# Filling one edge tile's source columns on a second engine (ScalarE, one group in 24) in place of its gather

## The chip, the cores and the metric

The kernel runs on one core of one Trainium2 chip. The metric is device time in microseconds (us). The core's engines appear in the profile as PE (TensorE matmul), PEld (its weight load), DVE (VectorE), ACT (ScalarE), POOL (GpSimd) and SP (SyncE, which issues DMAs). Each works off its own queue of instructions in order, and they wait for one another on semaphores.

## The reference

One layer of a message-passing graph network over N = 12500 nodes with 64 features and E = 212500 edges, which come sorted by destination. Everything is fp32.

```
msg_in   = concat(x[src], x[dst], edge_attr)            # 64 + 64 + 32
messages = relu(msg_in @ mW1 + mb1) @ mW2 + mb2
agg      = segment_sum(messages, dst, N)
u        = relu(concat(x, agg) @ uW1 + ub1) @ uW2 + ub2
out      = layernorm(x + u)
```

## The kernel before

**Tiles and groups.** The edges are cut into tiles of 128 and groups of three tiles (384 edges), which makes G = 554 groups. As the edges are sorted, the destinations of a group lie in a window of 32 nodes. A second path for inputs that break this is in the program behind a branch and isn't taken here.

**A group's path.** `gather(g)` (L143, POOL) issues one indirect DMA for each tile: it brings the 64 features of the 128 sources into a slot of the ring `own.s` (20 slots, one edge per partition). `onehot(g)` (L322, DVE) writes beside them, for each edge, which of the 32 window nodes it goes to. Then three PE parts follow. `turn(g)` (L352) transposes the three tiles into PSUM, and ScalarE copies the result to `own.st` (L364), where the 32 edge features of the group have been loaded below it (L282, SP). `hidden(g)` (L384) multiplies this with the weights `own.wm`, whose middle 32 rows hold the window's share (`windows`, L308 and L313), and ScalarE's relu writes `own.h` (L393). `sums(g)` (L411, L414) sums the messages of the window with the one-hot columns, and VectorE adds the sums to `agg` (L423) and the counts to a row of `xc` (L424), the table of all nodes with features on partitions.

**The order of work.** It is written out by hand. Iteration k of the main loop issues, in this order: on SP some loads; every fourth time the next four windows (`places`, L294 and L301 on DVE); `onehot(k + 1)`; one PE step that holds `turn(k)`, `hidden(k - 2)` and `sums(k - 4)`, and every fourth time the windows' matmul, followed by ScalarE's copy of k and relu of k - 2, and VectorE's sums of k - 4; `gather(k + 16)`; and `copies_of(k)`. The last instruction of a PE step alone raises the semaphore that the copy, the relu and the sums wait for. PSUM holds two steps, so that step k + 2 starts when VectorE has read step k. The first gather of a group waits until ScalarE's copy of the group 20 before it has freed the ring's slot. Every 512 finished nodes an update round (L441 to L475) is put between the steps, 25 in all.

**The copied tile.** In every 16th group from 44 on (`COPIED`, 31 groups), the last tile isn't gathered. VectorE copies its sources' columns out of `xc`, one node at a time, into `own.f` (L341: 64 partitions by 1 element), over the 16 iterations that end four before the group's own (`SPREAD`, `LEAD`): eight columns in an iteration, after eight indices have been loaded into registers (L336, one TENSOR_LOAD for eight). This tile needs no transposing of features: `hidden` multiplies `own.f` and the 32 lower rows separately (two matmuls in place of one), and the copy to `own.st` is made in two pieces, 64 rows by 256 and 32 rows by 384:

```
parts = [(slice(0, D + W), n)]
if g in COPIED:
    parts = [(slice(0, D), n - P), (slice(D, D + W), n)]
```

Of the kernel before, what the change touches and what calls it, by code (L numbers as in the profile page):

```python
# [13 lines left out]
AF = mybir.ActivationFunctionType  # L14
ALU = mybir.AluOpType
ET = mybir.EngineType
# [3 lines left out]
P = 128  # L20
N = 12500
E = 212500
D = 64
# [8 lines left out]
G = (E + GE - 1) // GE  # L32
# [10 lines left out]
BITS = 16  # L43
NEAR_GROUPS = 24
SHORT = 10
EVERY = 16
COPIED = range(44, G - 16, EVERY)
ONE = TG - 1
SPREAD = 16
LEAD = 19  # L50
REGS = 8
TIMES = 4

# [1 line left out]
def tiles_of(g):  # L55

    n = min(GE, E - g * GE)
    return [min(P, n - j * P) for j in range((n + P - 1) // P)]
# [23 lines left out]
class Own:  # L82
# [4 lines left out]
    def __init__(self, nc, ctx):  # L87
        def on(name, *shape, of=nc.sbuf_tensor):
            return ctx.enter_context(of(name, list(shape), F32)).ap()

        self.s = [on(f"own_s{i}", P, TG, D + W) for i in range(RING)]
        self.st = [on(f"own_st{i}", P, SB * GE) for i in range(BLOCKS)]
        self.wm = [on(f"own_wm{i}", P, H) for i in range(NW)]
        self.h = [on(f"own_h{i}", P, TG, H) for i in range(NH)]

        self.f = [on(f"own_f{i}", P, P) for i in range(2)]
        self.ident = on("own_ident", P, P)
        self.counts = on("own_counts", D + W, G)

        self.ps = [on(f"own_ps{i}", P, 3, 512, of=nc.psum_tensor) for i in range(2)]  # L100
# [3 lines left out]
def ordered(ctx: ExitStack, tc: tile.TileContext, a, own, ok):  # L104
# [3 lines left out]
    nc = tc.nc  # L108
# [9 lines left out]
    def copied(g, j):  # L118
        return g in COPIED and j == ONE

# [3 lines left out]
    nc.sync.dma_start(src_sb[:, :first], a["src"][:, :first])  # L124

    loads, places_by, copy_by, relu_by, sums_by, wm_by, turn_by = ({} for _ in range(7))
    efs_by, hidden_by, columns_by, ahead = {}, {}, {}, []

    def after(first, *others):

        tc.declare_no_dep(first.ins, group="quiet", reason="waits for the last of a step")
        for i in others:
            tc.add_manual_dep(
                first.ins, i.ins.name,
                mybir.DependencyInfo(mybir.DependencyClass.Sync, mybir.DependencyReason.DATA),
                reason="the kernel's own rings",
            )
        return first
# [27 lines left out]
    zero = const.tile([P, NP // P], F32, name="zero")  # L166
    nc.vector.memset(zero, 0.0)
    nc.vector.tensor_copy(ident, ident_t)
    for t in own.f:
        nc.vector.memset(t[D:, :], 0.0)  # L170
    iota = iop.tile([P, W], F32, name="iota")
    nc.vector.tensor_copy(iota, iota_i)
# [2 lines left out]
    xc = const.tile([D + 2, NP], F32, name="xc")  # L175
# [24 lines left out]

    cols_sb = const.tile([len(COPIED), P], I32, name="cols_sb")
    nc.sync.dma_start(cols_sb, a["src_rows"])
# [82 lines left out]
    def columns(g):  # L285
        t, c = own.st[g // SB % BLOCKS], (g % SB) * GE
        return t, c, sum(tiles_of(g))
# [31 lines left out]
    def onehot(g):  # L319
# [5 lines left out]
        )  # L325
        after(places_by[g], *([sums_by[g - RING]] if g >= RING else []))

    def copies_of(k):

        for i, g in enumerate(COPIED):  # L330
            at = k - (g - LEAD)
            if not 0 <= at < SPREAD:
                continue
            for r in range(at * P // SPREAD, (at + 1) * P // SPREAD):
                if r % REGS == 0:
                    _, ahead[:] = nc.values_load_multi_w_load_instructions(  # L336
                        cols_sb[i : i + 1, r : r + REGS], engines=[ET.DVE], min_val=0,
                        max_val=N - 1,
                        skip_runtime_bounds_check_because="a source is one of the nodes",
                    )  # L340
                c = nc.vector.tensor_copy(own.f[i % 2][:D, r : r + 1],  # L341
                                          xc[:D, bass.ds(ahead[r % REGS], 1)])
                after(c, *([hidden_by[COPIED[i - 2]]] if i > 1 else []))
                columns_by[g] = [c]

    def turn(g, ps):
# [9 lines left out]
        def copy(step):  # L356
            t, c, n = columns(g)
            turn_by[g] = step
# [3 lines that stand above are left out]
# [11 lines left out]
    def hidden(g, ps):  # L373
        t, c, n = columns(g)
        sizes = tiles_of(g)
        pre = ps[:, 1, : TG * H].rearrange("p (j h) -> p j h", h=H)
        did, w = [], wm[g % NW]
        for j, p in enumerate(sizes):
            cols = t[:, c + j * P : c + j * P + p]
            parts = [(cols, w)]  # L380
            if copied(g, j):
                parts = [(own.f[COPIED.index(g) % 2], w), (cols[D:, :], w[D:, :])]
            for i, (edges, weights) in enumerate(parts):
                did.append(nc.tensor.matmul(pre[:p, j, :], edges, weights, start=i == 0,  # L384
                                            stop=i == len(parts) - 1))
        needs = [copy_by[g], wm_by[g], efs_by[g // SB], *(wm_loads[g] if g < NW else ()),
                 *columns_by.pop(g, [])]

        def relu(step):
            hidden_by[g] = step  # L390
            h = own.h[g % NH]
            if len(set(sizes)) == 1:
                relu_by[g] = [nc.scalar.activation(h, pre, AF.Relu)]  # L393
            else:
                relu_by[g] = [nc.scalar.activation(h[:p, j, :], pre[:p, j, :], AF.Relu)
                              for j, p in enumerate(sizes)]
            for i in relu_by[g]:
                after(i, step, *([sums_by[g - NH]] if g >= NH else []))
            return relu_by[g]

        return did, needs, relu
# [80 lines left out]
    def step_update(g):  # L482
# [5 lines left out]
        elif now:  # L488
            got = now[1](now[0])
            now = [got, *now[2:]] if len(now) > 2 else []  # L490

    users = {part: [[], []] for part in (turn, hidden, sums)}

    def step(*work):
# [33 lines left out]
    for k in range(G):  # L528
        if k < BITS:
            bit(k)  # L530
        if k % SB == 2:
            inputs(k // SB + 2)
        if k % SB == 1:
            places(k // SB + 1)
        onehot(k + 1)
        if k < G - SHORT:
            step((turn, k), *([(hidden, k - 2)] if k > 1 else []),
                 *([(sums, k - 4)] if k > 3 else []))
            made, summed = max(0, k - 1), max(0, k - 3)
        else:  # L540

            step((turn, k))
            for _ in range(2):
                if summed < made:
                    step((sums, summed))
                    summed += 1
            for _ in range(2):
                if made <= k:
                    step((hidden, made))
                    made += 1  # L550
        if k + AHEAD < G:
            gather(k + AHEAD)
        copies_of(k)
# [285 lines left out]
@with_exitstack  # L839
def gnn_layer(ctx: ExitStack, nc, a):  # L840
    own = Own(nc, ctx)
    tc = ctx.enter_context(tile.TileContext(nc))
    flag = ctx.enter_context(tc.tile_pool(name="flag", bufs=1))
    ok = flag.tile([1, 1], I32, name="ok")
    with tc.manual_schedule():
        ordered(tc, a, own, ok)
    good = nc.values_load(ok[0:1, 0:1], min_val=0, max_val=1,
                          skip_runtime_bounds_check_because="a comparison's result")
    with tc.If(good == 0):
        with tc.manual_schedule():  # L850
            unordered(tc, a)
# [36 lines left out]
```

## Time and profile before

| | |
|---|---|
| three runs | 2655.7, 2661.27, 2664.23 us; median 2661.27 |
| the profiled execution | 2655.7 us; its span, first to last instruction, 2654.0 us |
| mean granted TensorE clock | 0.786 of full speed |
| busy share of the span | PE 64%, POOL 58%, PEld 55%, DVE 40%, ACT 21% |
| gathers (L143) | 1630, 944 ns each |
| columns copied (L341) | 3968, 144 ns each |

In the profile's rows, "idle before" is the time for which the engine did nothing just ahead of the instruction, with the event that ended it behind an arrow; "issue" there means that the profile shows no event for it. A matmul in fp32 counts as two instructions. The timeline's rows give the start, the duration, the engine, the line, the operation, the tiles, and how many instructions were merged into one row; a merged row's duration is that of all of them.

### The profile page before, as it was taken

How to read it: one execution, taken by the hardware profiler on the slowest of the kernel's cores; microseconds unless marked ns; L12 is line 12 of the kernel's file. 1: busy time of each engine (PE TensorE's matmuls, PEld its weight loads, DVE VectorE, ACT ScalarE, POOL GpSimd, SP SyncE). 2: the span in 40 equal slices, each digit the busy share in tenths (PEclk: the TensorE clock that was granted, in tenths of full speed). 3: DMA queues.
4: the chain of work that ended last, by engine and by line, in shares of the span. 5: the costliest groups of instructions: out<-in, count | busy, mean ns of one | idle time of the engine just before them, and what ended most of it. 6: DMA issues, size and time to landing. Idle time of an engine off the chain costs nothing. (4 is left out here: it accounts for less than half of the span.)

```text
span 2654.0 us, 39223 instructions
## 1 busy us (share of the span) xinstructions
PE 1694.0 (64%) x9503; PEld 1466.6 (55%) x9503; DVE 1061.8 (40%) x7161; ACT 563.0 (21%) x1746; POOL 1539.8 (58%) x1637
## 2 busy tenths in 40 slices
PE   0366666666666766666666766657666666666677
PEld 0355555555555655555565655556555555555565
DVE  4124344343443443434434434444344343443423
ACT  0112222221222221222212222222222222222222
POOL 7565555565555655565556555655555555565550
PEclk9677788777777877787877778887777878887779
DMA  3221111111111111111111111111111111111110
GB/s 75 59 46 37 35 33 38 30 37 32 36 34 35 33 37 31 37 33 35 37 33 36 34 34 34 35 35 34 36 32 38 31 37 32 36 35 35 35 33 15
DMA packets 72472, 95.61 MB, mean 36 GB/s; under 512 B 32956, under 2 KB 40378, under 8 KB 72234
## 3 DMA queue, kind: packets, MB, share of 16 engines
q0 software_dynamic: 52160, 53.49, 10.7%
q1 hardware_dynamic: 19160, 39.05, 5.3%
q8 instruction: 81, 1.33, 0.2%
q14 instruction: 157, 1.29, 0.2%
q10 hardware_dynamic: 914, 0.46, 0.1%
HBM read 89.58 MB, written 3.20 MB: 35 GB/s over the span
## 5 line engine op out<-in xcount | busy, mean ns | idle before, releaser
L143 POOL DMA_INDIRECT own_s<-in_x,src_sb x1630 | 1539.0, 944 | 1039.1 <-ACT own_st L364 584.1
L352 PE MATMUL own_ps<-own_ident,own_s 128*96 128x128 f32 x1661 | 373.0, 348 | 864.1 <-issue 737.4
L352 PEld LDWEIGHTS own_ps<-own_ident,own_s 128*96 128x96 f32 x1661 | 227.5, 161 | 943.6 <-issue 802.5
L364 ACT ACTIVATE own_st<-own_ps 96x384 f32<-96x384 f32 (+2 forms) x585 | 280.3, 479 | 1935.5 <-PE own_ps L414 1062.0
L414 PE MATMUL own_ps<-own_s,own_h 128*128 128x128 f32 x3322 | 654.3, 346 | 0.9 <-issue 0.9
L384 PE MATMUL own_ps<-own_wm,own_st 128*128 128x128 f32 (+1 forms) x3322 | 633.5, 341 | 1.4 <-DVE own_wm L313 1.4
L384 PEld LDWEIGHTS own_ps<-own_wm,own_st 128*128 128x128 f32 (+1 forms) x3322 | 582.3, 256 | 11.7 <-issue 6.3
L423 DVE TENSOR_TENSOR agg<-own_ps,agg 128x32 f32 x554 | 105.8, 191 | 1187.9 <-ACT own_h L393 1025.8
L414 PEld LDWEIGHTS own_ps<-own_s,own_h 128*128 128x128 f32 x3322 | 531.5, 238 | 27.9 <-issue 0.6
L341 DVE COPY own_f<-xc 64x1 f32 x3968 | 430.1, 144 | 216.6 <-issue 212.2
L393 ACT ACTIVATE own_h<-own_ps 128x384 f32<-128x384 f32 x553 | 264.3, 478 | 17.8 <-PE own_ps L384 13.0
L313 DVE COPY own_wm<-own_ps 32x128 f32<-32x128 f32 x550 | 157.0, 285 | 5.7 <-issue 0.2
L322 DVE TENSOR_TENSOR own_s<-iota,dlc 128x96 f32<-128x96 f32 x554 | 135.8, 246 | 13.7 <-issue 8.2
L424 DVE TENSOR_TENSOR xc<-own_ps,xc 1x32 f32 x554 | 101.1, 183 | 26.7 <-PE u_ps L442 5.1
L411 PE MATMUL own_ps<-own_ident,own_counts 32*1 32x32 f32 x554 | 107.2, 193 | 3.8 <-ACT own_st L364 1.9
L364 ACT ACTIVATION_READ_ACCUMULATOR own_st<-own_ps 96x1 f32 (+1 forms) x554 | 107.2, 194 | 0.7
L301 DVE COPY xw<-xc 66x32 f32 x554 | 76.3, 202 | 48.9 <-issue 45.5
L411 PEld LDWEIGHTS own_ps<-own_ident,own_counts 32*1 32x1 f32 x554 | 41.1, 74 | 95.1 <-issue 50.6
L454 PE MATMUL u_ps<-u,u 128*128 128x64 f32 (+1 forms) x196 | 49.1, 401 | 18.0 <-ACT u L444 15.6
L454 PEld LDWEIGHTS u_ps<-u,u 128*128 128x128 f32 (+1 forms) x196 | 47.2, 324 | 20.0 <-ACT u L444 17.2
L308 PE MATMUL own_ps<-w1b,xw 66*128 66x128 f32 (+1 forms) x276 | 57.2, 291 | 0.0
L308 PEld LDWEIGHTS own_ps<-w1b,xw 66*128 66x128 f32 (+1 forms) x276 | 45.7, 207 | 0.1
(62 smaller groups left out, 261.0 us busy)
## 6 DMA issues: line engine op xcount, KB each, us to landing
own_st<-in_efT SPq DMA_DIRECT2D x138, 192.0 KB
own_s<-in_x,src_sb POOLq DMA_INDIRECT x1630
xin<-in_x SPq DMA_DIRECT2D x24, 128.0 KB
out<-o SPq DMA_DIRECT2D x24, 128.0 KB
xc<-in_xT SPq DMA_DIRECT2D x12, 179.2 KB
dlc_i<-in_dst_cols SPq DMA_DIRECT2D x1, 831.0 KB
xc<-in_xT SPq DMA_DIRECT2D x4, 179.5 KB
src_sb<-in_src SPq DMA_DIRECT2D x13, 50.5 KB
```

Source lines behind the costliest of these rows:

```text
L143: nc.gpsimd.indirect_dma_start(out=s[:p, j, :D], out_offset=None, in_=x[:, :], in_offset=bass.IndirectOffsetOnAxis(ap=src_sb[:p, g * TG + ...
L308: did = nc.tensor.matmul(wp[: n * W, :], xw[:, :n, :], w1b, start=True, stop=True)
L313: c = nc.vector.tensor_copy(wm[g % NW][D : D + W, :], wp[i * W : (i + 1) * W, :])
L322: places_by[g] = nc.vector.tensor_tensor(own.s[g % RING][:, :, D:], iota.unsqueeze(1).to_broadcast([P, TG, W]), dlc[:, g * TG : (g + 1) * ...
L341: c = nc.vector.tensor_copy(own.f[i % 2][:D, r : r + 1], xc[:D, bass.ds(ahead[r % REGS], 1)])
L352: nc.tensor.transpose(xt[:, j * P : j * P + p], s[:p, j, :], ident[:p, :p])
L364: nc.scalar.activation(t[to, c : c + m], xt[to, :m], AF.Copy, **({"accum_out": counts[to, g : g + 1]} if to.stop > D else {})), step)
L384: did.append(nc.tensor.matmul(pre[:p, j, :], edges, weights, start=i == 0, stop=i == len(parts) - 1))
L393: relu_by[g] = [nc.scalar.activation(h, pre, AF.Relu)]
L411: did = [nc.tensor.transpose(line, counts[lo:, g : g + 1], ident[lo : D + W, lo : D + W])]
L414: did.append(nc.tensor.matmul(sg, h[:p, j, :], s[:p, j, D:].unsqueeze(1).to_broadcast([p, TIMES, W]), start=j == 0, stop=j == len(sizes) - 1))
L423: after(nc.vector.tensor_tensor(agg[:, at], sg[:, 0, :], agg[:, at], ALU.add), step),
```

## The change

A second set of groups is copied in place of gathered: every 24th from 48 on, 21 groups, none of which is in the first set. Their columns are copied by ScalarE, with an activation of the kind Copy, over the 24 iterations that end four before the group's own: 128 / 24, so five or six columns in an iteration, behind that iteration's relu in ScalarE's queue. ScalarE loads the indices into its own registers, eight at a time. Each engine has its own pair of tiles in `own.f`. VectorE's groups, and where its copies stand, stay as they were. The changed kernel has 1609 gathers, 3968 column copies on VectorE and 2688 on ScalarE, and 336 register loads on ScalarE.

```
-EVERY = 16
-COPIED = range(44, G - 16, EVERY)
 ONE = TG - 1
-SPREAD = 16
-LEAD = 19
+BY_DVE = range(44, G - 16, 16)
+BY_ACT = range(48, G - 16, 24)
+COPIED = {**dict.fromkeys(BY_DVE, (ET.DVE, BY_DVE)), **dict.fromkeys(BY_ACT, (ET.Activation, BY_ACT))}
+SLACK = 3
...
-        self.f = [on(f"own_f{i}", P, P) for i in range(2)]
+        self.f = {way: [on(f"own_f{len(way)}_{i}", P, P) for i in range(2)]
+                  for way in (BY_DVE, BY_ACT)}
...
+    def source_columns(g):
+        _, way = COPIED[g]
+        return own.f[way][way.index(g) % 2]
+
     def copies_of(k):
 
-        for i, g in enumerate(COPIED):
-            at = k - (g - LEAD)
-            if not 0 <= at < SPREAD:
+        for n, (g, (engine, way)) in enumerate(COPIED.items()):
+            at = k - (g - SLACK - way.step)
+            if not 0 <= at < way.step:
                 continue
-            for r in range(at * P // SPREAD, (at + 1) * P // SPREAD):
+            f, used, ahead = source_columns(g), g - 2 * way.step, held[engine]
+            for r in range(at * P // way.step, (at + 1) * P // way.step):
                 if r % REGS == 0:
                     _, ahead[:] = nc.values_load_multi_w_load_instructions(
-                        cols_sb[i : i + 1, r : r + REGS], engines=[ET.DVE], min_val=0,
+                        cols_sb[n : n + 1, r : r + REGS], engines=[engine], min_val=0,
                         max_val=N - 1,
                         skip_runtime_bounds_check_because="a source is one of the nodes",
                     )
-                c = nc.vector.tensor_copy(own.f[i % 2][:D, r : r + 1],
-                                          xc[:D, bass.ds(ahead[r % REGS], 1)])
-                after(c, *([hidden_by[COPIED[i - 2]]] if i > 1 else []))
+                column = f[:D, r : r + 1], xc[:D, bass.ds(ahead[r % REGS], 1)]
+                c = (nc.vector.tensor_copy(*column) if engine == ET.DVE
+                     else nc.scalar.activation(*column, AF.Copy))
+                after(c, *([hidden_by[used]] if used in way else []))
                 columns_by[g] = [c]
...
-                parts = [(own.f[COPIED.index(g) % 2], w), (cols[D:, :], w[D:, :])]
+                parts = [(source_columns(g), w), (cols[D:, :], w[D:, :])]
```

More of the change, by code (lines that the diff above doesn't have):

```diff
@@ L126, in ordered @@
     loads, places_by, copy_by, relu_by, sums_by, wm_by, turn_by = ({} for _ in range(7))
-    efs_by, hidden_by, columns_by, ahead = {}, {}, {}, []
+    efs_by, hidden_by, columns_by = {}, {}, {}
+    held = {ET.DVE: [], ET.Activation: []}
     def after(first, *others):
@@ L168, in ordered @@
     nc.vector.tensor_copy(ident, ident_t)
-    for t in own.f:
+    for t in [t for pair in own.f.values() for t in pair]:
         nc.vector.memset(t[D:, :], 0.0)
```

## The prediction

> **What bounds the kernel now.** I read the page's busy times and costliest groups first, then the waits, then the timeline of two stretches. The chain of waits covers only the last 100 us, so it says nothing about the loop.
>
> ```profile
> span 2654.0 us, 39223 instructions
> PE 1694.0 (64%) x9503; PEld 1466.6 (55%) x9503; DVE 1061.8 (40%) x7161; ACT 563.0 (21%) x1746; POOL 1539.8 (58%) x1637
> ...
> L143 POOL DMA_INDIRECT own_s<-in_x,src_sb x1630 | 1539.0, 944 | 1039.1 <-ACT own_st L364 584.1
> L352 PE MATMUL own_ps<-own_ident,own_s 128*96 128x128 f32 x1661 | 373.0, 348 | 864.1 <-issue 737.4
> ```
>
> No engine is full. PE idles 864 us ahead of its turns, and POOL idles 584 us for ScalarE's copy, so the gathers don't starve PE: counted over the trace's rows, PE's turn of a group starts about 84 us after the group's last gather was issued. Yet POOL matters, as the timeline shows:
>
> ```profile
> 1314.70 0.94 POOL L143 DMA_INDIRECT own_s<-in_x,src_sb  x1 [2.34 <-ACT own_st L364]
> ...
> 1319.68 0.94 POOL L143 DMA_INDIRECT own_s<-in_x,src_sb  x1 [0.30 <-issue]
> ...
> 1320.92 0.94 POOL L143 DMA_INDIRECT own_s<-in_x,src_sb  x1 [0.30 <-issue]
> 1320.98 0.94 PE L414 MATMUL own_ps<-own_s,own_h 128*128 128x128 f32 x6
> 1323.33 0.49 ACT L364 ACTIVATE own_st<-own_ps 96x384 f32<-96x384 f32 x1 [6.14 <-PE own_ps L414]
> ...
> 1324.17 0.94 POOL L143 DMA_INDIRECT own_s<-in_x,src_sb  x1 [2.31 <-ACT own_st L364]
> 1324.18 0.48 ACT L364 ACTIVATE own_st<-own_ps 96x384 f32<-96x384 f32 x1
> ...
> 1327.31 0.26 DVE L322 TENSOR_TENSOR own_s<-iota,dlc 128x96 f32<-128x96 f32 x1
> ...
> 1327.64 0.45 PEld L352 LDWEIGHTS own_ps<-own_ident,own_s 128*96 128x96 f32 x3 [5.92 <-issue]
> ```
>
> POOL issues six gathers, 1.25 us apart, and stops for the ring. Meanwhile PE has finished two steps, the first (with L308) at 1319.42 and the second at 1321.92, but ScalarE gets the first's signal only at 1323.33, some 1.4 us after POOL's last gather ended (1320.92 + 0.94). Counted over the trace's semaphore records: of the 244 steps whose matmuls ended 4 to 8 us into a streak of six gathers, 2 signalled at once; the others' signals came together about 8.6 us after the streak's start. Of 52 that ended in a streak's first 1.5 us, 50 signalled at once. Once the gathers are over, nothing is held:
>
> ```profile
> 2578.77 0.90 POOL L143 DMA_INDIRECT own_s<-in_x,src_sb  x1 [0.30 <-issue]
> ...
> 2581.84 0.94 PE L414 MATMUL own_ps<-own_s,own_h 128*128 128x128 f32 x6
> ...
> 2582.81 0.49 ACT L364 ACTIVATE own_st<-own_ps 96x384 f32<-96x384 f32 x1 [1.56 <-PE own_ps L414]
> ```
>
> So the loop is a lockstep. Two steps are released, POOL gathers two groups (7.2 us), the next signals come 1.4 us later, and copy and wake-up take 0.85. There are 276 such stalls for 554 groups, and between groups 60 and 520 a group takes 4.68 us. Inside this, a second loop runs nearly as long: release, copy, relu (1.0 us), VectorE's sums, its column copies, the one-hot (to 1327.57), PE's next turn (1327.64), whose step may end only at the streak's end.
>
> **Term 1, the gathers left out.** 21 gathers at 1.25 us are 26.2 us of POOL's time, if nothing else becomes late. The 31 tiles copied already show what is kept. I cut the trace at the turns of k divisible by 4; all copied groups, old and new, are divisible by 4. By how far ahead the copied group lies, four steps take 17.77 us (20 groups ahead: the streak with five gathers), 18.87 (24), 18.58 (28) and 19.56 (16, where another copied group is itself turned). Against 18.72, the mean of the two neutral cycles, a missing gather saves 0.95 us: 21 x 0.95 = -20 us.
>
> **Term 2, the copied group's own step.** The cycle of 19.56 loses 0.84. The rows explain it: ScalarE's copy comes in two pieces (376 and 482 ns for one of 485) on the path to the release, and PE makes four instructions in place of two for that tile (2 x 394 + 2 x 465 for 2 x 339 ns, 1.04 us more). 21 x 0.84 = +18 us. Terms 1 and 2 thus nearly cancel. With 27 cycles of each kind and a spread of 1.4 us, each mean is good to 0.27, so their sum is -2 +- 8 us.
>
> **Term 3, the columns on ScalarE.** 2688 copies and 336 register loads are spread over 504 iterations: 5.33 copies each, and a load in two of three. No such copy is in the trace on ScalarE. From below, VectorE's spacing holds, eight in 0.95 us, so 0.12 each; from above, ScalarE's smallest ACTIVATE (L463, 297 ns), nothing overlapped. I take about 0.15, nearer to the lower row, since ScalarE's read of the accumulator already starts 0.1 us before its copy's recorded end. A register load costs VectorE 0.9 us between its neighbours (L424's end to the next L341) and here about 0.75, as part of it runs under the relu. An iteration's block is thus 0.9 us (six, no load) to 1.5 us (five with a load); at the upper row 1.8 to 2.2.
>
> What is queued behind the block is the next step's copy and relu, and behind these POOL's ring and VectorE's sums. Where two signals come together, the second copy moves from 0.85 us after the release to between 1.7 and 2.4. POOL asks for it after three more gathers, 0.85 + 3.75 = 4.6 us (3.35 if the streak has lost one): covered. VectorE asks for the second relu once it is through with sums (0.4), columns (1.85) and one-hot (0.25) of the first, from 1.0 on: 3.5 us after the release. The relu is done at 0.85 + 0.9 to 1.5 + 0.97 = 2.7 to 3.3. So the cover is VectorE's own column block, and 0.2 to 0.8 us of it are left. In windowed steps 1.2 us more of L313 cover it; in a stretch without VectorE's columns the block would show whole. The stalls scatter by about 0.6 us (1.5 to 2.8 between their tenth and ninetieth percentile), so I let one in four of the 168 second steps that have a load be late by 0.3 us: +13 us. With the upper row 168 steps would be late by about 0.45 us: +76. From below it is 0: I see no gain in it, as nothing is taken off an engine that others wait for.
>
> [...]
>
> **Edits at nothing.** ScalarE's first column waits for the DMAs of `xc`; the last of these was issued at 148 us, and iteration 21 starts near 177. Two more tiles to clear (165 ns each) lie in VectorE's first 50 us, while PE has not begun; if that cover were gone, they would cost 0.3 us once. SP issues the same DMAs, `src_rows` with 21 more rows. Copy and Relu share the one table load of L364, so no reload comes. In update rounds ScalarE waits for L461, and the columns follow; VectorE is 3 us behind there.
>
> **Sum.** 2655.7 - 20 + 18 + 13 = 2667 for an execution like the profiled one, which is 5.6 us below the median of the runs; against that median the forecast is 2672 us, 0.4% slower. About 0.3% (8 us) is what can be told from no change here.
>
> **Rivals.** (1) Faster: the lockstep takes every gather at its price and ScalarE's block stays hidden. For it: POOL's 1630 x 1.25 us and 276 stalls of 1.95 make up nearly all its 2575 us. Against it: the 0.84 us of term 2. With -26, and half of term 2, it gives 2661 - 26 + 9 = 2644 us; it decides if an iteration's block stays under 1 us. (2) The change moves nothing measurable: terms 1 and 2 cancel and term 3 is 0 to 5 us, 2655 to 2669, because PE's steps just after a release (at half clock, 1327.67 to 1331.55) already end as late as a shortened streak. (3) Clearly slower: a copy from a register's address costs ScalarE about 0.3 us, and the second relu passes VectorE's 3.5 us; 2661 - 2 + 76 = 2735 us. It decides from 0.2 us per copy on.
>
> **Chances and range.** Forecast, small loss from a partly covered block: 0.34. Rival 1: 0.28. Rival 2: 0.23. Rival 3: 0.15. The forecast's case is near the line of 0.3% and reaches below it about as often as rival 2 reaches above, so slower is 0.34 + 0.15 = 0.49, same 0.23, faster 0.28. The forecast's own range is 2662 to 2695. To hold 8 in 10 it goes down through most of rival 1 and up to the middle of rival 3: 2638 to 2722.
>
> **What would show it.** Right: L143 with 1609 issues and some 270 stalls still ended by L364; column rows on ScalarE spaced 0.12 to 0.2 us; VectorE's idle time at L423 for L393 about as before; own-step cycles near 19.5 us in 21 more places. Term 1 is wrong if four-step cycles with five gathers don't fall by about 1 us; term 2, if the groups at 48 + 24i turn without a loss; term 3, if VectorE's waits for L393 grow by over 50 us, or if PE's start after a release moves. The whole is wrong if the 1.43 us between a streak's end and the held signals changes.

## The result, and the profile after

The changed kernel takes 2692.14 us (median of four runs, 2689.86 to 2694.34), against 2662.75 for the kernel before (four runs, 2655.7 to 2664.7): ratio 1.0115, 95% interval 1.0093 to 1.0137, so 29 us slower. The profiled execution took 2690.72 us, its span is 2688.9, which is 34.9 more than before. The page has these lines:

```profile
span 2688.9 us, 45023 instructions
PE 1687.1 (63%) x9545; PEld 1457.1 (54%) x9545; DVE 1060.2 (39%) x7163; ACT 827.3 (31%) x4455; POOL 1519.4 (57%) x1616
...
L145 POOL DMA_INDIRECT own_s<-in_x,src_sb x1609 | 1518.6, 944 | 1091.0 <-ACT own_st L372 677.1
L360 PE MATMUL own_ps<-own_ident,own_s 128*96 128x128 f32 x1661 | 364.2, 341 | 906.5 <-issue 677.0
...
L350 ACT ACTIVATE own_f<-xc 64x1 f32 x2688 | 304.6, 193 | 9.1 <-issue 6.2
```

POOL has 21 gathers fewer, worth 26 us at their spacing of 1.25, and yet ends later: what it waits for ScalarE's copies has grown from 584 to 677 us (part of that is only booked differently: the waits under "issue" fell from 448 to 410). Counted over the gaps between gathers, the stalls went from 538 us in 276 to 599 us in 284: +61 - 26 = +35, the whole of the difference between the two spans. ScalarE has room for its columns (L350): it is busy for 31% of the span. The timeline shows how short their block is:

```profile
1317.05 0.65 ACT L350 ACTIVATE own_f<-xc 64x1 f32 x6
...
1317.60 0.47 ACT L372 ACTIVATE own_st<-own_ps 96x384 f32<-96x384 f32 x1
```

Six columns take 0.65 us, one every 0.093, and the next copy starts in the shadow of the last. The Trainium skill's price for such an ACTIVATE (ScalarE: Activation LUTs, What ACT_TABLE_LOAD costs: 186 ns, 93 of it overlapped) agrees with these 193 ns each, 93 ns apart.

The lockstep is still there. These are two gathers, the end of a PE step beside them, and the copy that waits for that step, in the timeline of the changed kernel:

```profile
1330.23 0.94 POOL L145 DMA_INDIRECT own_s<-in_x,src_sb  x1 [0.30 <-issue]
...
1331.35 0.94 PE L422 MATMUL own_ps<-own_s,own_h 128*128 128x128 f32 x6
1331.48 0.94 POOL L145 DMA_INDIRECT own_s<-in_x,src_sb  x1 [0.30 <-issue]
1333.94 0.87 ACT L372 ACTIVATE own_st<-own_ps 64x256 f32<-64x256 f32 x2 [5.84 <-remote]
```

The step's matmuls end at 1332.29, and the copy starts at 1333.94, 1.52 us after the end of the last gather's issue (1332.42). This copy is one in two pieces, 0.87 us in place of 0.49.

### The profile page after: what moved, and what is told of

The parts are those of the page before. It is cut to its first block, busy times and chain, and to the rows that moved or that the text cites. A ratio compares the mean times of both kernels' runs of the same rounds, so it can differ in the third digit from the quotient of the medians.

```text
span 2688.9 us, 45023 instructions
## 1 busy us (share of the span) xinstructions
PE 1687.1 (63%) x9545; PEld 1457.1 (54%) x9545; DVE 1060.2 (39%) x7163; ACT 827.3 (31%) x4455; POOL 1519.4 (57%) x1616
## 4 chain that ended last, share of the span: by engine, by line
PE 50%; issue 18%; another core or an unknown queue 16%; ACT 10%; ACTq 3%; DVE 3%; DMA 0%; DVEq 0%; SPq 0%
PE own_ps L422 19%; PE own_ps L392 16%; PE own_ps L360 9%; ACT own_h L401 3%; ACT own_f L350 3%; ACT own_st L372 3%; ACTq L343 2%; PE own_ps L419 2%; PE u_ps L462 2%; PE u_ps L449 1%; PE own_ps L310 1%; ACTq L350 1%; PE u_ps L450 1%; DVE agg L431 1%
## 5 line engine op out<-in xcount | busy, mean ns | idle before, releaser
L145 POOL DMA_INDIRECT own_s<-in_x,src_sb x1609 | 1518.6, 944 | 1091.0 <-ACT own_st L372 677.1
L360 PE MATMUL own_ps<-own_ident,own_s 128*96 128x128 f32 x1661 | 364.2, 341 | 906.5 <-issue 677.0
L372 ACT ACTIVATE own_st<-own_ps 96x384 f32<-96x384 f32 (+2 forms) x606 | 286.1, 472 | 1697.7 <-PE own_ps L422 1006.0
L422 PE MATMUL own_ps<-own_s,own_h 128*128 128x128 f32 x3322 | 647.5, 343 | 0.4 <-issue 0.3
L392 PEld LDWEIGHTS own_ps<-own_wm,own_st 128*128 128x128 f32 (+1 forms) x3322 | 571.9, 251 | 16.5 <-issue 11.7
L431 DVE TENSOR_TENSOR agg<-own_ps,agg 128x32 f32 x554 | 105.2, 190 | 1202.7 <-ACT own_h L401 1089.6
L422 PEld LDWEIGHTS own_ps<-own_s,own_h 128*128 128x128 f32 x3322 | 525.6, 236 | 27.3 <-issue 0.3
L350 ACT ACTIVATE own_f<-xc 64x1 f32 x2688 | 304.6, 193 | 9.1 <-issue 6.2
```

Source lines behind the costliest of these rows:

```text
L145: nc.gpsimd.indirect_dma_start(out=s[:p, j, :D], out_offset=None, in_=x[:, :], in_offset=bass.IndirectOffsetOnAxis(ap=src_sb[:p, g * TG + ...
L350: else nc.scalar.activation(*column, AF.Copy))
L360: nc.tensor.transpose(xt[:, j * P : j * P + p], s[:p, j, :], ident[:p, :p])
L372: nc.scalar.activation(t[to, c : c + m], xt[to, :m], AF.Copy, **({"accum_out": counts[to, g : g + 1]} if to.stop > D else {})), step)
L422: did.append(nc.tensor.matmul(sg, h[:p, j, :], s[:p, j, D:].unsqueeze(1).to_broadcast([p, TIMES, W]), start=j == 0, stop=j == len(sizes) - 1))
```

## The experiments

Line numbers in the lines below are those of each kernel. "Theory" letters are those of the texts on record. In all experiments the kernel before takes some 2062 us beside them, not 2663: they ran on three chips (numbers 1, 6 and 11) other than the one of the first comparison, and this turned out to matter more than anything in the change.

**One part at a time.** Four kernels cut from the changed one:

```
e1_columns_only:  copied(g, j) and the two pieces test "g in BY_DVE", not "g in COPIED";
                  hidden(g) waits for columns_by only if g in BY_DVE
e2_tiles_only:    copies_of: + "or way is BY_ACT" in the test that skips an iteration;
                  own.f is cleared whole (memset(t, 0.0), not t[D:, :])
e3_gathers_only:  copies_of as in e2, copied(g, j) and the two pieces as in e1;
                  gather() still leaves the 21 tiles out
e4_whole_copy:    - if g in COPIED:
                  -     parts = [(slice(0, D), n - P), (slice(D, D + W), n)]
```

> ScalarE fills the 21 tiles' columns as in the changed kernel, but the tiles are also gathered, and turned and multiplied as gathered tiles: the columns are never read. Theory A (the copied group's own step, with its two-piece copy and its extra matmuls, costs more than the gather left out gives): no change from before, ratio 0.998 to 1.003, as the columns run 0.093 us apart in ScalarE's idle time. Theory B (ScalarE's columns hold up the next step's copy and relu): most of the 29 us of the changed kernel, ratio 1.008 to 1.02.

> The 21 tiles are not gathered and go the copied tile's way (two-piece copy, two matmuls for one), but nobody fills their columns; left out are ScalarE's 2688 copies and 336 register loads, and with them the source features of these tiles, which count as zero. Theory A: as slow as the changed kernel, ratio 1.008 to 1.015. Theory B: terms 1 and 2 of the prediction alone, -2 +- 8 us, ratio 0.996 to 1.002.

> Only the 21 gathers are left out; the tiles are turned, copied in one piece and multiplied once, with whatever features the ring's slot held, and no columns are filled on ScalarE. This is term 1 of the prediction alone. If a gather's time counts as the cycles of before say, -20 us, ratio 0.992; at its full price -26 us, ratio 0.990. If the lockstep takes nothing back for it, 1.000. Theory A asks for a gain here that its own step then more than eats; theory B says nothing of it.

> The changed kernel, but ScalarE copies all 96 rows of all three tiles in one piece for the 52 copied groups too; the third tile's feature columns are then never read. This takes 0.38 us off the path to the release in 52 groups, 31 of which were in the kernel before. Theory A: 52 x 0.38 = 20 us off the changed kernel, ratio to before 1.002 to 1.007. Theory B: less, as the hold-up sits elsewhere: 0 to 20 us off, ratio up to 1.011.

On this chip the kernel before takes 2062.43 us, not 2662.75. Ratios to it: columns only 0.9997 (0.9988 to 1.0006); tiles only 0.9873 (0.9858 to 0.9889); gathers only 0.9877 (0.9862 to 0.9892); whole copy 0.9876 (0.9861 to 0.9891). Whatever leaves out 21 gathers is 25 to 26 us faster, and nothing else in the change can be seen at all: the three kernels are within 1 us of one another, and e1 is level with the kernel before. The page of the first (with all 1630 gathers) and its timeline say why:

```profile
span 2059.5 us, 44940 instructions
...
L145 POOL DMA_INDIRECT own_s<-in_x,src_sb x1630 | 1539.0, 944 | 497.8 <-issue 367.3
```

```profile
1315.92 0.94 POOL L145 DMA_INDIRECT own_s<-in_x,src_sb  x1 [0.30 <-ACT own_h L401]
1316.02 0.94 PE L422 MATMUL own_ps<-own_s,own_h 128*128 128x128 f32 x6
1317.00 0.49 ACT L372 ACTIVATE own_st<-own_ps 96x384 f32<-96x384 f32 x1 [0.62 <-PE own_ps L422]
1317.16 0.94 POOL L145 DMA_INDIRECT own_s<-in_x,src_sb  x1 [0.30 <-issue]
```

PE's step ends at 1316.96 in the middle of running gathers, and the copy starts 0.04 us later. By the semaphore records no step's signal came more than 0.02 us late here (591 steps); on the first chip 379 of 575 came more than 0.1 us late. POOL never stalls after the first ten us, issues a gather every 1.25 us from end to end (1630 x 1.25 = 2037 us), and PE's turn of a group starts 2.9 us (median) after the issue of its last gather began, not some 84. Here POOL is the bound.

**The changed kernel there.** No edit.

> The changed kernel itself, as it stands. The first four experiments ran on a chip on which the kernel before takes 2062 us, not 2661: there no PE signal is held while gathers run, POOL issues its gathers without a stall, and leaving out 21 of them gave the full 25 to 26 us. If the sign of the change hangs on whether the signals are held (theory C): ratio 0.985 to 0.990 where the kernel before takes about 2062 us, and about 1.01 where it takes about 2661. If the changed kernel loses for a reason of its own on every chip (theories A and B): over 1.005 on either.

On another such chip: 2036.5 us against 2061.97, ratio 0.9873 (0.9856 to 0.9889). The same program is 1.15% slower on the one chip where signals are held and 1.27% faster on this one, where they aren't. Theory C fits both; A and B fail as statements about every chip, and are left as statements about the held lockstep.

**Bringing the hold back.** No later run fell on the first chip. So a wait was added to the kernel before and to cuts of the changed one (l1: changed, l2: e1, l3: e2, l4: e3): ScalarE's copy of every even group g from 20 on also waits until the last gather of group g + 19 has landed. The gathers are emitted three iterations sooner to make it expressible:

```
+                if g % 2 == 0 and to is parts[0][0] and 20 <= g < G - RING:
+                    after(copy_by[g], loads[g + RING - 1][-1])
...
+        for g in ([AHEAD, AHEAD + 1, AHEAD + 2] if k == 0 else []) + [k + RING - 1]:
+            if g < G:
+                gather(g)
...
-        if k + AHEAD < G:
-            gather(k + AHEAD)
```

> The kernel before, with one wait added: ScalarE's copy of every even group k also waits until the last gather of group k + 19 has landed, as the profile of before showed PE's signals to be held until a streak of gathers had landed. (The gathers are emitted three iterations earlier for this; their order in POOL's queue and the waits on the ring stay.) On a chip that holds no signals this should bring back the lockstep: 2 groups per streak of six, 7.2 us + 1.4 + 0.85, so about 4.7 us a group, 2580 to 2680 us, with some 260 to 280 stalls. If it stays under 2200, the lockstep was not what made that chip slow.

> The changed kernel with the same added wait; to be set against the kernel before with it. Theory C1 (held signals alone turn the change from a gain into a loss): slower than it by 10 to 40 us. Theory C2 (the loss on the first chip came from something else that chip does): the 21 gathers count at their full price, about 26 us faster than it.

> The added wait, and ScalarE's 2688 columns filled but never read; the 21 tiles are gathered too. Theory B within C1 (ScalarE's block before the second copy of a pair makes the loss; in the trace of the first chip the neutral four-step cycles of the changed kernel stall 4.20 us and not 3.70): slower than the kernel before with the wait by 10 to 50 us. Theory A: within 5 us of it.

> The added wait, the 21 tiles not gathered and taken the copied way, but no columns filled on ScalarE, whose source features thus count as zero. Theory A within C1 (the copied group's own step eats the gather): no faster than the kernel before with the wait, 0 to +20 us. Theory B: -10 to -26 us.

> The added wait, and only the 21 gathers left out: these tiles are turned, copied in one piece and multiplied once with whatever the ring's slot held, and no columns are filled on ScalarE. If the copied group's own step ate the gather in the held runs (theory A): 15 to 26 us below the kernel before with the wait (2747), so 2721 to 2732. If the lockstep itself takes the 1.25 us back, because PE's two steps set the next release and not the gathers (theory D): 2740 to 2755.

Ratios are to the kernel before without the wait (2062 to 2064 us):

| kernel with the wait | median us | ratio (95%) |
|---|---|---|
| l0, before | 2747.13 | 1.3322 (1.3300 to 1.3344) |
| l1, changed | 2750.99 | 1.3335 (1.3313 to 1.3357) |
| l2, columns only | 2755.65 | 1.3354 (1.3332 to 1.3376) |
| l3, tiles only | 2755.16 | 1.3338 (1.3316 to 1.3361) |
| l4, gathers only (another chip) | 2720.48 | 1.3191 (1.3169 to 1.3213) |

The one wait turns 2062 us into 2747, with 263 stalls. The lockstep is back as expected, but the time is 67 us above the expected 2580 to 2680 and 84 above the first chip's. Copies that wait for the running gathers are thus enough to make a kernel this slow. The wait is a stand-in, though: it holds ScalarE's copies of a fixed half of the groups, not PE's signals. It also answers one rival, a slower clock: the granted TensorE clock was 0.786 on the first chip and about 0.91 on these, and in l0 it is 0.778 on a chip of the latter kind, so the low clock can come with the lockstep rather than cause it. The page of l0 is like that of the first chip:

```profile
span 2742.3 us, 39235 instructions
...
L143 POOL DMA_INDIRECT own_s<-in_x,src_sb x1630 | 1539.3, 944 | 1127.4 <-ACT own_st L364 696.2
```

Within it, three things follow; each ratio is good to about 4.5 us, so each difference to some 6. A gather left out by itself pays in full even in the lockstep: l4 is 27 us below l0, 1.27 us for each (21 us by the spans of the two profiled executions). The copied tile's own way takes that back: l3, with the same 1609 gathers, is 30 us above l4 by the ratios (35 by the medians), some 1.5 us a tile. And ScalarE's columns cost 7 to 9 us beside l0 (l2; the intervals just overlap) but nothing beside l3 (l1, which has them, is no slower), so their price here is not clear of the noise. The pages of l4 and l3 show the second in POOL's wait for the copies:

```profile
L145 POOL DMA_INDIRECT own_s<-in_x,src_sb x1609 | 1519.7, 945 | 1126.1 <-ACT own_st L372 706.9
```

```profile
L145 POOL DMA_INDIRECT own_s<-in_x,src_sb x1609 | 1519.9, 945 | 1157.6 <-ACT own_st L372 737.9
```

706.9 us in l4, 737.9 in l3. The changed kernel with the wait comes out level with l0 (+1.3 in a thousand, inside both intervals), neither the 10 to 40 us slower of theory C1 nor the 26 faster of C2. So the added wait reproduces that the 26 us disappear, but not that 29 more are lost.

**Where the tile's own way bites.** Cutting the traces into cycles of four steps, as the prediction did, and adding up POOL's stalls in each, shows one kind of cycle that the kernel before doesn't have. A group's own step and the streak that lacks a gather belong to different groups, 20 apart. With groups at 44 + 16i alone they never fall into the same cycle. With 48 + 24i added they do, 20 times (48 + 24i = 44 + 16j +- 20). Such cycles stall 5.7 and 5.6 us on the first chip (9 of either kind between groups 64 and 520, good to 0.2), where other cycles with an own step stall 4.4 to 4.5. In the kernels with the wait it is 6.1 against 5.1 to 5.4, in l1 and l3 alike. In l4 the 21 tiles have no own way: the cycles in which such a tile is turned while an older group's gather is missing are at 5.05, while the other kind, an older copied group's step beside a new missing gather, stays at 6.2.

The meetings are only part of it. Set against l4, l3 stalls 1.0 us more in the nine meetings in which one of the 21 tiles is turned (6.07 against 5.05), and still 0.7 more in the ten cycles in which one is turned without a meeting (5.06 against 4.38). Together these are 16 of the 27 us by which l3's stalls exceed l4's between groups 64 and 520; the rest lies in cycles in which none of the 21 is turned, and is not explained. A meeting on the first chip:

```profile
1337.78 0.94 POOL L145 DMA_INDIRECT own_s<-in_x,src_sb  x1 [0.30 <-ACT own_f L350]
1339.03 0.94 POOL L145 DMA_INDIRECT own_s<-in_x,src_sb  x1 [0.30 <-issue]
1339.12 0.85 PE L360 MATMUL own_ps<-own_ident,own_s 128*96 128x128 f32 x3 [6.83 <-issue]
...
1340.27 0.94 POOL L145 DMA_INDIRECT own_s<-in_x,src_sb  x1 [0.30 <-issue]
...
1340.61 0.63 PE L392 MATMUL own_ps<-own_wm,own_f 128*128 128x128 f32 x2
1341.17 0.79 PE L392 MATMUL own_ps<-own_wm,own_st 64*128 64x128 f32 x2
...
1342.04 1.65 PE L422 MATMUL own_ps<-own_s,own_h 128*128 128x128 f32 x6
...
1343.72 0.49 ACT L372 ACTIVATE own_st<-own_ps 96x384 f32<-96x384 f32 x1 [6.28 <-PE own_ps L422]
...
1344.57 0.94 POOL L145 DMA_INDIRECT own_s<-in_x,src_sb  x1 [3.35 <-ACT own_st L372]
```

The streak of five ends at 1341.21, a gather sooner than usual. But the next release is that of the step which multiplies the copied tile in two pieces (four instructions, 1.42 us), its matmuls end at 1343.69, and POOL waits 3.35 us. In this cycle the gather's 1.25 us are waited off.

**More tiles on ScalarE.** The whole copy of e4, with ScalarE's groups at 46 + 12i (41 groups) and 46 + 8i (62):

```
-BY_ACT = range(48, G - 16, 24)
+BY_ACT = range(46, G - 16, 12)          # e7_act_every_8: 8
```

> As e4_whole_copy, with ScalarE's groups at 46 + 12i: 41 of them, 11 columns an iteration. Where POOL's gathers set the time (theory C, chips that hold no signals), 41 gathers fewer than before are 51 us: ratio 0.975, about 2011 us. Where signals are held: no gain, 1.00 to 1.02.

> The same at 46 + 8i: 62 groups, 16 columns an iteration, about 1.5 us of ScalarE beside some 1 us of copy and relu in a group of then 3.54 us. If POOL still bounds: 77 us off, ratio 0.9625, about 1985 us. If ScalarE's two register loads and 16 copies an iteration now hold up copy and relu: between 0.97 and 1.0. Where signals are held: 1.01 to 1.04.

On a chip that holds no signals: 2012.33 us, ratio 0.9763 (0.9746 to 0.9779), and 2004.40 us, ratio 0.9710 (0.9686 to 0.9735). The first gains what 41 gathers cost (50 of 51 us); the second 58 of 77. POOL does save the 77: it never stalls, and its last gather starts at 1960.6 us, against 2037.5 in e1. But PE's turns fall behind the gathers, from some 9 us around group 60 to 37 around group 480, and 42 us of work follow the last gather where 22 did. The likely reason, which no run isolates, is that ScalarE fills up: its page has ACT busy for 1345.2 of the span's 2002.6 us, and it idles another 263 us ahead of its columns, without an event that ends the wait; I take these for register loads:

```profile
L350 ACT ACTIVATE own_f<-xc 64x1 f32 x7936 | 871.2, 193 | 269.4 <-issue 263.1
```

The last is the fastest version here, ahead of both kernels; it was not run where signals are held.

## Why the prediction was right or wrong

**The reading of the bound holds up, for the chip that the profile came from.** Waits like the hold of PE's signals behind running gathers, which was worked out from the trace, make a 2062 us kernel into a 2747 us one when they are put in by hand. What the profile couldn't show is that the hold isn't the kernel's: on the three other chips it is absent. There the change gains rival 1's -26 us, though not for rival 1's reason, as there is no lockstep; and the ratio of 0.987 lies outside the stated range, which is 0.991 to 1.023 of the median before.

**On the first chip sign and range held; the size, +11 us, was a third of +29.** The sign was partly luck. In the forecast, terms 1 and 2 nearly cancel and the loss is ScalarE's block, term 3; that block turned out shorter than assumed, and no run ties the 29 us to it. By the terms:

- Term 1 (-20) was a little small: a gather alone is worth 1.27 us in the lockstep (l4), so -26 to -27.
- Term 2 (+18) was too small, if l3 against l4 is its measure: held, the own way costs 30 to 35 us for 21 tiles. I had read the 0.84 us off a kernel in which own steps and shortened streaks never meet, and took terms 1 and 2 to be independent. The new groups' place was in the diff: had I laid 48 + 24i over 44 + 16j, shifted by 20, the 20 meetings could have been counted ahead. But they don't account for all that is missing: in the cycles in which one of the 21 tiles is turned, l3's extra over l4 is 16 us for 19 tiles, 0.84 each, just what term 2 had.
- Term 3 (+13) stood on a wrong block: 0.5 to 0.75 us where I put 0.9 to 1.5. The copies are 0.093 us apart, not 0.15, and ScalarE idles only 9.1 us in all ahead of its 2688 columns (the row of L350), so its 336 register loads hardly show. The 0.9 us that I had read for a load on VectorE was a misreading too: from L424's end to the next L341 it is 0.57 us (median of 372). What the block costs when held, between nothing and 7 to 9 us, stays within the noise.
- The three measured when held, -27, +30 to 35 and at most 9, would add up to some +3 to +17; the changed kernel itself is at +3 to 4 over l0, good to 6. Neither reaches the first chip's 29.
- Two of my own tests came out against me. VectorE's waits for relu grew by 64 us (L423 and now L431, below), more than the 50 at which I called term 3 wrong; with so short a block I take the growth for the later releases, which is argued and not shown. And the time from a streak's end to the copy that it releases did change, from 1.40 to 1.51 us on average (median 1.43 to 1.50).

```profile
DVE agg L423 <- ACT own_h L393: 1025.8, 275, 46.3
```

```profile
DVE agg L431 <- ACT own_h L401: 1089.6, 280, 47.6
```

**The account of the 61 us on the first chip.** The average stall after its release is 0.03 us longer (0.908 to 0.936 from the copy to POOL's restart): 284 x 0.028 = 8 us, the second pieces of 21 copies (0.37 us each). The release itself comes 0.11 us later: 31 us. Eight stalls more are some 17. This says where the time lies, not why the releases come later. Seen by cycles between groups 64 and 520, the 18 meetings account for some 25 of 58 us there, the rest is spread over all kinds of cycle, those without any tile of ScalarE in them too (neutral ones stall 4.21 us, before 3.85, each good to 0.1; the 3.70 in l2's text is too low). In the kernel before, some of that chip's signals slipped through early in a streak and broke up the pairs; in the changed one the stalls sit more on the even groups (457 us of 518, before 341 of 461). Why fewer slip through, and whether the columns do it, stays open: the added wait fixes which signals are held, so l2 couldn't show it, and no later run fell on the first chip.

## What to carry to other kernels

Before costing an edit from one profile, ask whether the bound in it is the program's or the machine's: here POOL, which stalled for a fifth of one chip's trace (538 of 2654 us), was the bound on the others, and the same edit changed sign. Where work is moved at two periods, lay the periods over each other and over the ring's length, and count where one edit's extra work meets another's saving; a price measured where they never meet need not hold where they do. A saving ahead of a wait is only kept if the next release is not itself late.

## What the runs showed of the hardware

On the first chip a PE step that ended well inside a streak of gathers was signalled only when the gathers had landed, 1.4 us after the last one's issue ended and up to some 4 us after the step. VectorE's and ScalarE's signals were not held there: PE's turns started 0.10 us after the one-hot that they waited for, and VectorE's sums 0.03 us after the relu (medians of 220 and 345 waits). On the three chips of the experiments there is no such delay: 0.02 us at most in 591 steps of e1, and in e5 and e7 at most one step of 659 over 0.1 us. The kernel before runs in 2062 instead of 2661 us there.

The first chip's trace is also thin. Each gather raises its semaphore 16 times when it lands; of these 26080 events the trace of the kernel before holds 8209, and of VectorE's 2098 it holds 1281. In e1's trace 25986 of the 26080 are there, and all of VectorE's. So PE's late signals may be one sign of something wider, in which the recording of the events could itself have a part. No run separates the chip from its state at that time or from the recording, and what makes the difference stays open.

ScalarE copies a column of 64 by 1 from an address in a register every 0.093 us. VectorE's columns come 0.103 us apart on average: three in four some 0.115 (eight in 0.95 us), the others 0.06 to 0.07 (eight in 0.57 us). For these single-column copies ScalarE is thus about as fast as VectorE.
